# Four generator units per visit, lower products three tiles behind, and one adapter visit per block in a four-stage float32 kernel

## The chip, the cores and the metric

The kernel runs on one core of a Trainium2 chip. The metric is device time in microseconds (us) from launch to end: the median of several runs. One further run was taken under the hardware profiler; all durations below come from that one. The core has five engines that run side by side, each with its own queue worked through in order: PE (matrix products), DVE (vector), ACT (scalar functions), POOL (a second vector engine, which also issues stores here) and SP, which only issues DMA transfers.

## The reference

4096 tokens of width 256 (64 sequences of 64), a condition vector of 64 numbers per sequence, and four layers in a row. Cut to what matters:

```python
# layer 0: normed, gated up product, then quantized ternary down product
h = x * ((cond @ norm_w.T + 1)[:, None] * rsqrt(mean(x*x) + 1e-6))
val, gate = split(h @ up_w.T)                  # up_w: 2048 x 256
y = act_quant(val * gelu(gate)) @ weight_quant(down_w).T + x
# layer 1: attention and a gated MLP, both scaled by vectors made of the condition
x = x + (t @ attn_alpha_w.T)[:, None] * attention(ada_rmsnorm(x, t, attn_gamma_w, attn_beta_w))
x = x + (t @ ffn_alpha_w.T)[:, None] * swiglu(ada_rmsnorm(x, t, ffn_gamma_w, ffn_beta_w))
# layer 2: layer norm plus tanh(condInfo @ lin_w.T + lin_b)
# layer 3: an adapter whose two weights are generated for each sequence
Wd_b = Wd + ((h_lang @ Wdd.T + bdd) * 0.1).reshape(B, 128, 256)
Wu_b = Wu + ((h_lang @ Wdu.T + bdu) * 0.1).reshape(B, 256, 128)
out  = x + relu(x @ Wd_b.T + bd) @ Wu_b.T + bu
```

The generated weights are 64 times two matrices of 32,768 numbers: 16.8 MB of generator weights are read, and as much is written to device memory and read back.

## The kernel before

Precision is kept by splitting each float32 operand of a large product into a high and a low part; `mm3` (lines 81 to 85) makes three products of them. Apart from SP's, the order of each engine's work is the order in which the program is written out: whatever the Python loop emits first comes first in that engine's queue. SP's order is chosen by a scheduler. Tiles come from pools with a fixed number of buffers per tag; taking a buffer again waits for its last reader.

**Stage 0** (`l0`, lines 288 to 507) runs over 32 tiles of 128 tokens, eight blocks of four. For tile `n`, `upper(n, 0)` and `upper(n, 1)` each make 12 products of 128x512 into two of the eight PSUM banks (tag `mm`), then ACT's gelu (line 395) and a DVE product (396). `quant(n)` (399) is five DVE instructions and a DMA transpose issued by SP into `qt`. `lower(n)` (412) is eight bf16 products from `qt` and two DVE instructions. In the loop at line 473 `lower` is two tiles behind `upper`, with tiles 0 and 1 both at `n == 3`. `ternary` and `ternary_rest` (321, 326) quantize the down weights at `n` 1 and 2; a DVE sum of two ACT results is line 328, and PE's line 330 needs it.

Beside that the stage does the **generator**, 32 units: `gen_load` (257, SP loads 512 KB into one of four `gt` buffers), `gen_make` (266, four products of 64x64 weights by 512 columns into two banks) and `gen_store` (277, two ACT copies into one of two `stg` buffers, two stores issued by POOL). Two units are made before the loop, then two per even tile.

`cond_rest` (134, a hook of tile 4) makes seven condition vectors: 14 products of 64 rows (line 116) and two of 256 columns (151), all on partitions 0 to 63.

**Attention** follows and is not touched. **The last stage** (line 1066 on) runs over 64 visits, `n = 8*i + f` for block `i`: `f_inner(n)` is 24 products of 128x512, `f_outer(n - 2)` 12 of 128x256, each with ACT and DVE work between. For the next block, `f_load`, `f_begin` (ACT squares, line 210, and a POOL root) and `f_scale` (four ACT instructions, line 225) run at `f` 2, 3 and 4, and PE's transposes of the result (line 234) at 5 and 6. For the block before, the adapter's down product `f_down(i - 1)` (858, 64 records on PE) is at `f == 6` and its up product `f_up_products(i - 1)` (873) at `f == 7`. Both use the two `mm` banks of this stage. `f_weights` loads the generated weights at `f == 6`. The last block's adapter is in `f_last`.

The loop of stage 0 and its ends are what the change moves most:

```python
                if n % 2 == 0 and n > 0:
                    gen_make()
                    gen_make()
                    gen_load()
                    gen_load()
                    gen_store()
                    gen_store()
...
            if n == 3:
                lower(0)
            if n >= 3:
                lower(n - 2)
```

Of the kernel before, what the change touches and what calls it, by code (L numbers as in the profile page):

```python
# [28 lines left out]
X1 = 5  # L29
# [7 lines left out]
def tile_kernel(ctx: ExitStack, tc, xT, x, condT, cw, upT, downT, qkvT, woT, ghT, outT_w,  # L37
# [87 lines left out]
    def cond_load():  # L125
        nc.sync.dma_start(out=vc, in_=vecs)
        bo = crest["bo"] = main.tile([NB, D], F32, tag="xg", bufs=2, name="bo")
        nc.sync.dma_start(out=bo, in_=rows[0:1, :].broadcast_to([NB, D]))
        for v0 in (1, 5):
            n = min(4, 8 - v0)  # L130
            cwt = crest[v0] = main.tile([64, 4, D], F32, tag="x1", bufs=X1, name=f"cwt{v0}")
            nc.sync.dma_start(out=cwt[:, :n], in_=cw[:, v0:v0 + n, :])

    def cond_rest():
        part = const.tile([P, 1], mybir.dt.int32, name="part")
        nc.gpsimd.iota(part, pattern=[[0, 1]], base=0, channel_multiplier=1)
        pbit = const.tile([P, 1], mybir.dt.int32, name="pbit")
        nc.vector.tensor_scalar(pbit, part, 16, None, ALU.bitwise_and)
        pf = const.tile([P, 1], F32, name="pf")
        nc.vector.tensor_copy(pf, pbit)  # L140
        nc.vector.tensor_scalar(par[:, 1:2], pf, 1.0 / 16.0, None, ALU.mult)
        nc.vector.tensor_scalar(par[:, 0:1], pf, -1.0 / 16.0, 1.0, ALU.mult, ALU.add)
        nc.vector.tensor_tensor(w2, vc[:, 1, :], vc[:, 1, :], ALU.mult)
        bo = crest["bo"]
        al = main.tile([NB, 3, D], F32, tag="xn", bufs=1, name="al")
        pbs = [bank("mm") for _ in range(3)]
        for v0 in (1, 5):
            for v in range(v0, min(v0 + 4, 8)):
                cond_vector(crest[v0][:, v - v0], pbs[v0 // 5], 2 * NB * (v - v0))
        for i, v in enumerate((V_AA, V_FA)):  # L150
            nc.tensor.matmul(pbs[2][:NB, i * D:(i + 1) * D], lhsT=ct[0:64], rhs=crest[1 + 4 * i][:, v - 1 - 4 * i],
                             start=True, stop=True)
        src = [pb.rearrange("p (v c b) -> p v c b", c=2, b=NB) for pb in pbs]
        nc.vector.tensor_copy(cv[:, 1:5], src[0])
        nc.vector.tensor_copy(cv[:, 5:7], src[1][:, 0:2])
        nc.vector.tensor_copy(al[:, 0:2], pbs[2][:NB].rearrange("b (i d) -> b i d", i=2))

        th = main.tile([P, 2, NB], F32, tag="st", bufs=2, name="th")
        for c in range(2):
            nc.scalar.activation(th[:, c], src[1][:, 2, c], AF.Tanh, bias=vc[:, 3, c:c + 1])  # L160
        nc.vector.tensor_tensor(al[:, 2], al[:, 1], bo, ALU.mult)
        nc.gpsimd.dma_start(out=alphad.rearrange("v b d -> b v d"), in_=al)
        for c in range(2):
            nc.vector.tensor_scalar(th[:, c], th[:, c], vc[:, 2, c:c + 1], vc[:, 1, c:c + 1], ALU.add, ALU.mult)
            nc.vector.tensor_scalar(cv[:, V_LIN, c], th[:, c], vc[:, 2, c:c + 1], None, ALU.add)
# [88 lines left out]
    gen_left = [(g, sd, k) for g, sd in ((g1, s1d), (g2, s2d)) for k in range(16384 // (2 * GC))]  # L254
    gen_loaded, gen_made = [], []

# [19 lines left out]

    def gen_store():
        if gen_made:
            pb, dst = gen_made.pop(0)
            uid[0] += 1  # L280
            stg = pools["a"].tile([P, 2, GC], F32, tag="stg", bufs=2, name=f"stg{uid[0]}")
            for s in range(2):
                nc.scalar.copy(stg[:, s], pb[s])
            for c in range(2):
                nc.gpsimd.dma_start(out=dst[:, :, c * GC:(c + 1) * GC], in_=stg[c * 64:(c + 1) * 64])


    def l0(hooks):
# [32 lines left out]
        def ternary():  # L321
            for j in range(2):
                wj = main.tile([P, 4, D], F32, tag="xn", bufs=1, name=f"wj{j}")
                nc.scalar.activation(wj, til["wd"][j], AF.Abs, accum_out=sa[:, j:j + 1])

        def ternary_rest():
            wd, ones = til.pop("wd"), til.pop("ones")
            nc.vector.tensor_tensor(sb[:, 0:1], sa[:, 0:1], sa[:, 1:2], ALU.add)
            pb = bank("mm")
# [69 lines left out]
        def quant(n):  # L399
            h = til[n]  # L400
            am = pool.tile([P, 4], F32, tag="am", bufs=4, name=f"am{n}")
            nc.vector.tensor_reduce(am[:, 0:1], h, AX.X, ALU.max, apply_absolute_value=True)
# [4 lines left out]
            nc.vector.tensor_scalar(q, h, -MAGIC, 127.0, ALU.add, ALU.min)  # L407
            qt = pool.tile([P, 8, P], BF16, tag="qt", bufs=3, name=f"qt{n}")
            nc.sync.dma_start_transpose(out=qt, in_=q)
# [26 lines left out]
        load_up(3, nc.sync)  # L436
        gen_load()
        load_up(1, nc.sync)
        gen_load()
        til["ones"] = pool.tile([P, P], F32, name="ones")  # L440
# [18 lines left out]
        nc.vector.tensor_scalar(gl, ct, 0.1, None, ALU.mult)  # L459
        gen_make()  # L460
        gen_make()
        for j in (3, 1):
# [4 lines left out]
        upper(1, 0, "rest")  # L467
        gen_store()
        gen_store()
        gen_load()  # L470
        gen_load()
        N = NBLK * TT
        for n in range(N + 2):
            if n < N:
                if n > 1:
                    upper(n, 0)
                if n % 2 == 0 and n > 0:
                    gen_make()
                    gen_make()
                    gen_load()  # L480
                    gen_load()
                    gen_store()
                    gen_store()
# [18 lines left out]
            if n < N - 1:  # L502
                quant(n)
            if n == 3:
                lower(0)
            if n >= 3:
                lower(n - 2)

# [286 lines left out]

    def f_weights(i):

        pool = pools["c"]
        B = fblk[i]
        B["wd"], B["wu"] = [], []  # L800
        for k in range(2):
            bs = slice(i * BB + 4 * k, i * BB + 4 * k + 4)
            wd = pool.tile([P, 4, 2, BN], F32, tag="wd", bufs=4, name=f"wd{i}_{k}")
            for c in range(2):
                nc.sync.dma_start(out=wd[:, :, c, :], in_=s1d[c, bs].rearrange("b d n -> d b n"))
            wu = pool.tile([P, 4, D], F32, tag="wu", bufs=4, name=f"wu{i}_{k}")
            for s in range(2):
                nc.sync.dma_start(out=wu[s * 64:(s + 1) * 64], in_=s2d[s, bs].rearrange("b n d -> n b d"))
            B["wd"].append(wd)
            B["wu"].append(wu)  # L810

# [51 lines left out]

    def f_up_products(i, half=None):
        B = fblk[i]
        b0, b1 = (0, BB) if half is None else (half * BB // 2, (half + 1) * BB // 2)
        pus = []
        for c in range(2):
            pu = bank("mm" if half is None else "gh")
            for b in range(b0, b1):  # L870
                for s in range(2):
# [4 lines left out]
                                     tile_position=(0, 64 * s))  # L876
            pus.append(pu)
        return pus

    def f_up_store(i, pus, half=None):  # L880
        B = fblk[i]
        if half in (None, 0):
            B["yo"] = pools["c"].tile([P, 2, T], F32, tag="yo", bufs=1, name=f"yo{i}") if i + 1 < NBLK else \
                main.tile([P, 2, T], F32, tag="xn", bufs=1, name=f"yo{i}")
        yo, n = B["yo"], T if half is None else T // 2
        o = 0 if half is None else half * n
        for c in range(2):
            nc.vector.scalar_tensor_tensor(yo[:, c, o:o + n], pus[c][:, :n], vc[:, 4, c:c + 1], B["x4"][:, c, o:o + n],
# [177 lines left out]
    for n in range(5, N):  # L1066
        i, f = divmod(n, 8)
        ahead = 0 < i < NBLK - 1

# [8 lines left out]
        if i > 0 and f in (4, 5):  # L1078
            f_adapt(i - 1, f - 4)
        if i + 1 < NBLK and f in (5, 6):  # L1080
            late = [norm_turn(*fblk[i + 1]["n"], i + 1, f - 5, V_FG, V_FB)]
        if ahead and f == 6:
            f_down(i - 1)
        if ahead and f == 7:
            pus = f_up_products(i - 1)
        f_parts(n, sg)
        f_outer(n - 2) if n > 5 else None
        if ahead and f == 7:
            f_up_store(i - 1, pus)
        if n == 6:  # L1090
            for k in range(2):
                nc.vector.scalar_tensor_tensor(bias[:, k], gbt[:, 2 * k + 1], 0.1, gbt[:, 2 * k], ALU.mult, ALU.add)
        if i > 0:
# [5 lines left out]
            if f == 2:  # L1099
                f_center(i - 1, range(TT), rln)  # L1100
        if f == 2 and i > 0:
            f_rows(i)
            if i + 1 < NBLK:
                f_load(i + 1)
        if i > 0 and i + 1 < NBLK:
            if f == 3:
                f_begin(i + 1)
            if f == 4:
                f_scale(i + 1)

        if f == (6 if i + 1 < NBLK else 2):
            f_weights(i)
        if i + 1 < NBLK and f == 7:
            f_common(i, "wd", 0)
# [3 lines left out]
        if i > 0 and f in (3, 4):  # L1118
            f_common(i - 1, "wu", f - 3)
        if i + 1 == NBLK:  # L1120
            if f == 4:
# [61 lines left out]
```

## Time and profile before

| | us |
|---|---|
| three runs | 772.38, 776.98, 777.23 (median 776.98) |
| the profiled run | 779.7 |
| its span, from first to last instruction | 777.9 |
| stage 0, to the first attention products | about 282 |
| DVE busy, whole span | 545.4 (70%) |
| ACT busy | 398.8 (51%) |
| POOL busy | 336.8 (43%) |

The profile has a page of sums, and the trace behind it answers questions: busy time of each engine by stretch, with the clock that PE was granted; the list of who waited for whom; and each engine's instructions in order of time. In a row of such a list, the first number is the start in us, the second how long it took (several equal instructions in a row are merged, `x16` being their number), and the bracket at the end is the idle time before it and what ended it. A PE record's duration contains its way through the array; the pace of PE is the distance between the starts of neighbouring records. One float32 product of 64-row or 64-column tiles is two records.

### The profile page before, as it was taken

To read this page: it belongs to the slowest core of one execution; us is meant where nothing else is said; L and a number is where in the kernel's file an instruction comes from. 1 tells how busy PE (TensorE), PEld (TensorE's weight loads), DVE (VectorE), ACT (ScalarE), POOL (GpSimd) and SP (SyncE) were. 2 spreads that over 40 slices of the span, in tenths; PEclk is the share of its full clock that TensorE was granted. 3 is DMA by queue.
4 is the path that set the end of the run, shared out by engine and by line. 5 is a ranking of instruction groups with operands and counts; after the bars stand their busy time and mean duration, and the time that the engine had idled before them with its cause. 6 is when DMAs were issued, how large, how long until landed. Compare 5 with 4: busy or idle time off the path is not lost. (4 is left out here: it accounts for less than half of the span.)

```text
span 777.9 us, 17431 instructions
## 1 busy us (share of the span) xinstructions
PE 757.5 (97%) x7034; PEld 618.7 (80%) x7034; DVE 545.4 (70%) x863; ACT 398.8 (51%) x818; POOL 336.8 (43%) x348
## 2 busy tenths in 40 slices
PE   8989999999999999999999999999999999999997
PEld 5667767776776878888888888888888888888886
DVE  4868687786778689898889886555555555564665
ACT  6624355344354478888887674534444352526232
POOL 2312122221324336566655417381818272636491
PEclk9989999999999999999999999999999999999999
DMA  8966888987974774455654127726161617171601
GB/s 309 322 173 201 235 244 220 299 193 223 289 187 114 194 173 103 128 142 136 151 150 110 46 93 176 163 77 142 56 163 56 163 55 163 55 163 32 160 1 56
DMA packets 117184, 118.87 MB, mean 153 GB/s; under 512 B 39616, under 2 KB 100672, under 8 KB 117104
## 3 DMA queue, kind: packets, MB, share of 16 engines
q1 hardware_dynamic: 109104, 91.55, 48.1%
q0 software_dynamic: 7488, 25.37, 9.1%
q8 instruction: 55, 0.90, 0.5%
q10 hardware_dynamic: 512, 0.85, 0.4%
q14 instruction: 25, 0.20, 0.1%
HBM read 71.41 MB, written 29.56 MB: 130 GB/s over the span
## 5 line engine op out<-in xcount | busy, mean ns | idle before, releaser
L83 PE MATMUL mm<-up,xhl 128*128 128x512 f32 x256 | 107.2, 419 | 1.4 <-ACT xhl L217 1.4
L730 DVE TENSOR_TENSOR sg<-gh,sg 128x512 f32<-128x512 f32 x61 | 42.0, 689 | 93.5 <-ACT sg L729 47.4
L84 PE MATMUL mm<-up,xhl 128*128 128x512 f32 x256 | 102.5, 400 | 0.4 <-DVE up L313 0.4
L85 PE MATMUL mm<-up,xll 128*128 128x512 f32 x256 | 102.4, 400 | 0.0
L83 PE MATMUL gh<-xhf,gh 128*128 128x512 f32 x244 | 97.2, 399 | 0.0
L84 PE MATMUL gh<-xlf,gh 128*128 128x512 f32 x244 | 96.9, 397 | 0.0
L85 PE MATMUL gh<-xhf,gh 128*128 128x512 f32 x244 | 96.9, 397 | 0.0
L395 ACT ACTIVATE g<-mm,rs_l 128x512 f32<-128x512 f32 x64 | 43.9, 689 | 89.0 <-PE mm L85 65.3
L752 DVE TENSOR_TENSOR hlo<-sg,hhi 128x512 fp32r<-128x512 f32 x61 | 63.1, 1034 | 37.0 <-ACT hhi L751 36.6
L751 ACT CAST hhi<-sg 128x512 fp32r<-128x512 f32 x61 | 37.8, 620 | 84.7 <-DVE sg L730 83.8
L396 DVE SCALAR_TENSOR_TENSOR h<-mm,rs_l,g 128x512 f32<-128x512 f32 x64 | 47.5, 747 | 44.2 <-PE mm L85 43.1
L83 PE MATMUL acc<-wout,hhi 128*128 128x256 f32 x256 | 74.9, 293 | 0.0
L85 PE MATMUL acc<-wout,hlo 128*128 128x256 f32 x256 | 72.4, 283 | 0.3 <-DVE hlo L752 0.2
L84 PE MATMUL acc<-wout,hhi 128*128 128x256 f32 x256 | 72.3, 282 | 0.0
L83 PEld LDWEIGHTS mm<-up,xhl 128*128 128x128 f32 x256 | 49.2, 192 | 25.0 <-DVE am L404 4.9
L729 ACT ACTIVATE sg<-gh 128x512 f32<-128x512 f32 x61 | 36.0, 590 | 53.1 <-PE gh L85 53.1
L85 PEld LDWEIGHTS mm<-up,xll 128*128 128x128 f32 x256 | 48.8, 191 | 12.2 <-DVE xll L218 0.3
L84 PEld LDWEIGHTS mm<-up,xhl 128*128 128x128 f32 x256 | 49.2, 192 | 10.7 <-DVE up L313 0.9
L85 PEld LDWEIGHTS gh<-xhf,gh 128*128 128x128 f32 x244 | 46.1, 189 | 10.8
L238 POOL TENSOR_TENSOR xg<-xg,cv 128x512 f32<-128x512 f32 x32 | 35.8, 1128 | 42.9 <-DVE xg L237 42.9
L84 PEld LDWEIGHTS gh<-xlf,gh 128*128 128x128 f32 x244 | 46.3, 190 | 8.1
L83 PEld LDWEIGHTS gh<-xhf,gh 128*128 128x128 f32 x244 | 46.3, 190 | 8.1
(189 smaller groups left out, 1882.4 us busy)
## 6 DMA issues: line engine op xcount, KB each, us to landing
gt<-in_g SPq DMA_DIRECT2D x32, 512.0 KB, 5.8
rows<-alphad SPq DMA_DIRECT2D x48, 256.0 KB, 4.3
s1d<-stg POOLq DMA_DIRECT2D x32, 256.0 KB, 6.9
s2d<-stg POOLq DMA_DIRECT2D x32, 256.0 KB, 6.6
vb<-vx SPq DMA_DIRECT2D x32, 256.0 KB, 4.7
wd<-s1d SPq DMA_DIRECT2D x32, 256.0 KB, 4.5
wu<-s2d SPq DMA_DIRECT2D x32, 256.0 KB, 6.2
xt<-in_x SPq DMA_DIRECT2D x8, 512.0 KB, 5.3
```

Source lines behind the costliest of these rows:

```text
L83: nc.tensor.matmul(out, lhsT=l[0], rhs=r[0], start=first, stop=False)
L84: nc.tensor.matmul(out, lhsT=l[0], rhs=r[1], start=False, stop=False)
L85: nc.tensor.matmul(out, lhsT=l[1], rhs=r[0], start=False, stop=last)
L238: nc.gpsimd.tensor_tensor(b3(xg), b3(xg), bc(vb, c, i), ALU.add)
L395: nc.scalar.activation(g, pg, AF.Gelu, scale=rs[:, t:t + 1])
L396: nc.vector.scalar_tensor_tensor(h[:, ch * 512:(ch + 1) * 512], pv, rs[:, t:t + 1], g, ALU.mult, ALU.mult)
L729: nc.scalar.activation(sg, pg, AF.Silu)
L730: nc.vector.tensor_tensor(sg, pv, sg, ALU.mult)
L751: nc.scalar.copy(h_hi, sg)
L752: nc.vector.tensor_tensor(h_lo, sg, h_hi.bitcast(F32), ALU.subtract)
```

## The change

Generator: none is made before the loop; eight visits, at tiles 5, 8, 11, 15, 18, 22, 25 and 29, make four units each, with their ACT copies right behind (`gen_stage`, four staging buffers from two pools instead of two). Loads and stores are called once per tile (twice at some visits). `lower` runs three tiles behind instead of two. The condition weights lie on both halves of the partitions, and the products alternate between the halves. The sum of line 328 moves from tile 2 to tile 1. In the last stage the up product of block `i - 2` and the down product of block `i - 1` are one visit at `f == 7`, the down product between the two halves of the up product; preparation of the next block moves to `f` 0, 1 and 3, and weights are loaded at `f` 6 (down) and 7 (up).

```diff
+        cwt = crest["w"] = main.tile([P, 4, D], F32, tag="x1", bufs=X1, name="cwt")
+        nc.sync.dma_start(out=cwt[0:64], in_=cw[:, 1:5, :])
+        nc.sync.dma_start(out=cwt[64:128, 0:3], in_=cw[:, 5:8, :])
...
-        for v0 in (1, 5):
-            for v in range(v0, min(v0 + 4, 8)):
-                cond_vector(crest[v0][:, v - v0], pbs[v0 // 5], 2 * NB * (v - v0))
+        pbs = [bank("mm") for _ in range(4)]
+        for k in range(4):
+            for c in range(2):
+                for h in range(2 if k < 3 else 1):
+                    hs = slice(64 * h, 64 * h + 64)
+                    nc.tensor.matmul(pbs[h][:, (2 * k + c) * NB:(2 * k + c + 1) * NB],
+                                     lhsT=cwt[hs, k, c * P:(c + 1) * P], rhs=ct[hs], start=True, stop=True)
+        for h, k in ((0, V_AA - 1), (1, V_FA - 5)):
+            hs = slice(64 * h, 64 * h + 64)
+            nc.tensor.matmul(pbs[2 + h][:NB, :D], lhsT=ct[hs], rhs=cwt[hs, k], start=True, stop=True)
...
+    def gen_stage():
+            gen_turn.append(pools["kv"] if len(gen_turn) % 2 else pools["a"])
+            stg = gen_turn[-1].tile([P, 2, GC], F32, tag="stg" if len(gen_turn) % 2 else "qf", bufs=2,
                                    name=f"stg{uid[0]}")
             for s in range(2):
                 nc.scalar.copy(stg[:, s], pb[s])
+            gen_staged.append((stg, dst))
...
+            nc.vector.tensor_tensor(sb[:, 0:1], sa[:, 0:1], sa[:, 1:2], ALU.add)
...
         def ternary_rest():
-            nc.vector.tensor_tensor(sb[:, 0:1], sa[:, 0:1], sa[:, 1:2], ALU.add)
...
+        visits = (5, 8, 11, 15, 18, 22, 25, 29)
-                if n % 2 == 0 and n > 0:
-                    gen_make()
-                    gen_make()
+                if n in visits:
+                    for _ in range(4):
+                        gen_make()
+                        gen_stage()
+                for _ in range(0 if n == 0 else 2 if n in visits and (n + 3 in visits or n == visits[-1]) else 1):
                     gen_load()
-                    gen_load()
-                    gen_store()
                     gen_store()
...
-            if n == 3:
-                lower(0)
-            if n >= 3:
-                lower(n - 2)
+            if n > 3:
+                for k in range({4: 0, N + 1: N - 1}.get(n, n - 3), {N: N - 1, N + 1: N}.get(n, n - 2)):
+                    lower(k)
...
-        ahead = 0 < i < NBLK - 1
+        more = i + 1 < NBLK
...
-        if ahead and f == 6:
-            f_down(i - 1)
-        if ahead and f == 7:
-            pus = f_up_products(i - 1)
+        up = i - 2 if more and f == 7 else i - 2 if not more and f == 0 else -1
+        if up >= 0:
+            def between(pus):
+                f_up_store(up, pus, chunks=range(1))
+                if more:
+                    f_down(i - 1)
+            pus = f_up_products(up, between=between)
+            f_up_store(up, pus, chunks=range(1, 2))
+        elif more and i > 0 and f == 7:
+            f_down(i - 1)
...
+            if f == 0:
+                f_load(i + 1)
+            if f == 1:
+                f_begin(i + 1)
+            if f == 3:
+                f_scale(i + 1)
...
-        if f == (6 if i + 1 < NBLK else 2):
-            f_weights(i)
+        if f == (6 if more else 1):
+            f_weights(i, "wd")
+        if f == (7 if more else 1):
+            f_weights(i, "wu")
```

The two buffer counts that go with it: `am` 5 instead of 4, `qt` 4 instead of 3. The two `gen_load` calls between the first weight loads are gone.

## The prediction

> **What bounds the kernel.** First the table of busy time by stretch. Its columns are the stretch, then time on PE (records), PE's weight loads, DVE, ACT and POOL, the clock granted to PE, DMA share and GB/s.
>
> ```profile
> 40.00:60.00 20.00, 17.63 (x95) 12.47 (x93) 12.63 (x31) 3.96 (x8) 3.23 (x6) 0.84 0.68 172
> ...
> 120.00:160.00 40.00, 40.00 (x212) 28.83 (x213) 31.88 (x59) 16.78 (x34) 6.88 (x11) 1.00 0.87 242
> ...
> 560.00:600.00 40.00, 39.86 (x320) 34.52 (x320) 21.37 (x35) 16.61 (x35) 20.21 (x18) 1.00 0.42 106
> ```
>
> PE is full almost everywhere, so only two things can be won: PE's few waits, and PE time that does no work. From 40 to 60 us PE waits 2.4 us and its clock averages 0.84. Cut into single microseconds, the clock is at 0.50 or falling to it from 43.5 to 46.9 and from 57.1 to 60.5: twice 3.4 us at half pace, 1.7 us lost each time.
>
> Next, who PE and its weight loads waited for (total, times, longest):
>
> ```profile
> PE mm L421 <- DMA qt<-q: 2.4, 1, 2.4
> ...
> PE mm L330 <- DVE sb L328: 1.4, 1, 1.4
> ...
> PEld mm L234 <- ACT xnf L225: 3.1, 12, 0.3
> ```
>
> Then PE in order of time, at those waits and at the two kinds of narrow products:
>
> ```profile
> 42.85 1.33 PE L421 MATMUL mm<-wq,qt 128*128 128x256 bf16 x8 [2.37 <-DMA qt<-q]
> ...
> 53.06 3.34 PE L116 MATMUL mm<-ct,cwt 64*128 64x64 f32 x28
> 56.32 1.22 PE L151 MATMUL mm<-cwt,ct 64*64 64x256 f32 x4
> 57.48 1.89 PE L421 MATMUL mm<-wq,qt 128*128 128x256 bf16 x8
> ...
> 68.85 0.40 PE L85 MATMUL mm<-up,xll 128*128 128x512 f32 x1
> 69.17 1.95 PE L273 MATMUL mm<-gt,gl 64*64 64x512 f32 x16
> 71.05 0.50 PE L83 MATMUL mm<-up,xhl 128*128 128x512 f32 x1
> 71.39 0.39 PE L84 MATMUL mm<-up,xhl 128*128 128x512 f32 x1
> ```
>
> ```profile
> 591.67 0.60 PE L234 MATMUL mm<-ident,xnf 128*128 128x128 f32 x4
> 592.20 2.08 PE L858 MATMUL mm<-x,wd 128*64 128x64 f32 x64
> 594.21 0.38 PE L83 MATMUL acc<-wout,hhi 128*128 128x256 f32 x1
> 594.43 0.28 PE L84 MATMUL acc<-wout,hhi 128*128 128x256 f32 x1
> ```
>
> Going into narrow products and out again costs time beside the work. Wide 128x512 products start 0.233 us apart; from 68.85 to 71.39 is 2.54, less two wide steps 2.07. The sixteen records in it start in four groups, 0.43 apart, so the work is 1.72 and the switching **0.36**. From 591.67 to 594.43 is 2.76; four transposes at 0.108, 32 pairs of records at 0.058 and one product at 0.117 make 2.41, the rest is **0.35**.
>
> **The change, part by part.**
>
> *Generator visits.* Sixteen become eight; products, copies, loads and stores stay the same in number. 8 x 0.36 = **2.9** won. A visit of four takes 4 x 0.86 + 0.36 = 3.8 on PE, and its eight copies on ACT 8 x 0.515 = 4.1 (four merged are 2.06). A visit fills all eight banks. In the program, the last two units and the products after them wait for copies of the first three, one copy or so behind, and for DVE's reads of the tile. DVE, at 80% here, is at most one `quant` (3.1) behind while PE has two units (1.7) and the tile's own second half (2.8) to do. I take no wait; if PE had to stand until every copy is out, it would be 1.0 (first unit) + 4.1 - 3.8 = 1.3 a visit, 10.4 in all.
>
> The Trainium skill speaks against this part (TensorEngine Tiling (Array Packing), PSUM Bottleneck): tiling speeds TensorE but not the emptying of PSUM, whose copies can become the bound. By it the visits would run at the pace of the copies, 0.33 longer each, and the change would win 2.6 less.
>
> *Loads and stores.* In SP's order in the changed program the four loads of a visit stand almost together, behind the visit whose buffers they take; transposes queue behind them, but the next `lower` is then still two tiles (over 12 us) away, against 5.8 to land a load and 3.7 a transpose. The stores have two more staging buffers. At the start, two loads fewer stand ahead of the last up weights and four ahead of the down weights, so these only come earlier. 0.
>
> *Line 328 a tile earlier.* At tile 2 it stood behind `quant(1)` and two products on DVE. Now it waits there for ACT's two sums, which end near 24; PE asks near 28. The gap from 31.77 to 33.52 less one step: **1.5**.
>
> *`lower` three behind.* Tile 1's transpose gets one more tile, and the 2.37 wait goes: **2.4**. The half clock right behind it goes too: **1.7**.
>
> *Condition vectors.* From the last wide step (52.97) to 57.48 is 4.5. Single records start 0.112 apart, the four 256-column ones about 0.22. That quarters of the array run at once is shown by the generator's groups of four, which start within 0.02. Two halves at once: 14 x 0.112 + 2 x 0.22 + 0.5 for switching = 2.6, so **1.9** won (0 to 2.0).
>
> *A new wait, tiles 4 and 5.* Without the early generator work PE runs ahead of DVE. PE from 16.7: eight half tiles at 2.8, the `ones` product 0.2, condition 2.6, two `lower` 1.7: at 43.5 it wants a bank of `upper(4, 0)`. DVE from 20.3 without a pause: `quant(0)` 3.1, a product 0.7, the next block's split 2.8, `quant(1)` 3.1, two products 1.4, ternary 4.7, `quant(2)` 3.1, two products 1.4, `quant(3)` 3.1, one product 0.7: 44.4. **-0.9**. If the pairing saves nothing, PE comes 1.9 later and this wait is gone, so the two terms together are 0 to 2 and I take 1.0. Behind the wait stand the first generator visit and all of PE; from tile 8 on DVE has caught up.
>
> *The second half clock.* It came after some 4 us in which PE was never idle, but at most half of the array had work. Only 2.6 such us are left: **1.7**, or 0.
>
> The skill (TensorE: Matmul & The Clock Gate, Part 1) gives half rate as the state after an idle window of about 3.4 us. This trace differs: one drop came after 2.4 us of waiting, one after none. By the page, long visits could never cost clock.
>
> *Last stage.* Twelve adapter visits become seven: 5 x 0.35 = **1.8**. The up product's second half needs the bank of its first back: DVE finishes the inner product (0.7) and reads the bank (0.7) while PE spends 1.9 on the down product. The relu on ACT now waits for the up product's end, since `dn` has one buffer, and `hhi` stands behind it, 4 us late; `f_outer` reads that two visits (8 us) later. The normed rows (line 225) move to `f == 3`, a visit of 4.2 before PE's transposes instead of right ahead of them; ACT is 42% busy there and the POOL root is one visit earlier as well. The 3.1 of waits go: **3.1**. What is then latest is PE itself.
>
> Sum: 2.9 + 1.5 + 2.4 + 1.7 + 1.0 + 1.7 + 1.8 + 3.1 = **16.1**. From the profiled run's 779.7 (span 777.9) that makes 763.6 (761.8). The profiled run is 2.7 above the median of the plain runs, 776.98, so for those: **761**.
>
> **Rivals.**
>
> *Half of it* (0.14). The second drop stays (1.7), pairing brings nothing (1.0), and the normed rows' wait is replaced by another of its size in the last stage (3.1): 10.3 won, 767. For it: a block there has three DVE chains close to PE. Against: those rows alone are listed for PE's loads.
>
> *Banks bind* (0.08). PE stands until copies are out: 16.1 - 10.4 = 5.7 won, 771. For it: eight copies need 4.1 against PE's 3.8. Against: copies free banks one by one, and 15 waits of ACT for generator products (21.8 us) stand against two of PE for copies (1.6, weight loads only).
>
> *Long visits cost clock* (0.06), the slower case. A visit of 3.8 us and an adapter visit of 1.9 + 1.9 = 3.8 are both longer than the 3.4 us of a drop. If narrow tiles count as little work, each of the 8 + 7 is followed by half clock: 15 x 1.7 = 25.5, net 9.4 lost, 786. It decides from the tenth drop on (16.1 / 1.7). For it: the drop at 57.1 followed narrow products. Against: those used one half and were spaced by weight loads; generator records fill four quarters back to back, and no drop follows any of sixteen visits.
>
> *It does not do what it says*: the four loads are not spread over the tiles, as SP's order shows; that costs nothing by the sum above.
>
> **How the numbers follow.** The forecast has 0.72. The range reaches from 756 (no new wait, and a run like the 772.38 one) to 769 (half of it, and a little more): both first cases, about eight in ten. Runs before lie 4.9 apart, so 1% (7.8 us) is about what can be told from no change. Faster by more: 0.72 + 0.14 less 0.02 for drift = 0.84. Within 1%: the bank case and the drift, 0.10. Slower: 0.06.
>
> **What would show it.** Right: no PE wait for `qt` or `sb` and none of `xnf`; no 0.50 clock between 40 and 65; eight generator visits of 3.8; condition records starting in pairs; seven adapter visits; one PE wait near 1 us for DVE's `h` at tile 5; the first attention products some 10 us sooner. Wrong: PE waiting for `stg` at the visits, half clock behind them, or idle DVE while PE waits for `qt`.

## The result and the profile after

The changed kernel takes **768.89 us** (median of seven runs, 766.15 to 770.52). The kernel before, run beside it on the same chip, takes 773.41 (seven runs, 772.38 to 777.23). The ratio on record is 0.992, with a 95% interval of 0.9891 to 0.9949 (the quotient of the two medians is 0.994). The forecast was 761, with 769 as its upper end: the sign was right, but 0.8% was won where 2.1% was forecast. The profiled run of after took 768.89, its span 767.1.

The table of busy time by stretch, for the changed kernel, with the columns of the first table above:

```profile
40.00:60.00 20.00, 19.50 (x132) 13.40 (x131) 18.73 (x41) 8.94 (x17) 4.62 (x7) 1.00 0.62 171
120.00:160.00 40.00, 40.00 (x225) 27.87 (x224) 30.27 (x58) 20.49 (x46) 9.79 (x15) 1.00 0.95 244
200.00:240.00 40.00, 37.09 (x198) 25.20 (x200) 28.32 (x53) 18.63 (x47) 12.26 (x17) 0.96 0.90 206
560.00:600.00 40.00, 40.00 (x340) 35.21 (x339) 22.36 (x36) 16.83 (x36) 21.11 (x18) 1.00 0.48 114
```

The early stretch is mended: PE is busy for 19.50 of 20 us where it was 17.63, at a clock of 1.00 where it was 0.84. But a new hole stands at 200 to 240, where PE is short by 2.9 us and the clock is at 0.96. The list of waits names it:

```profile
PE mm L278 <- DVE x L435: 2.9, 2, 2.0
```

Line 278 is the generator's product, line 435 the last instruction of `lower` on DVE, which frees the bank that the generator wants. PE in order of time, first at the condition vectors, then at the visit of tile 25:

```profile
41.06 2.00 PE L152 MATMUL mm<-ct,cwt 64*128 64x64 f32 x28
42.98 0.65 PE L156 MATMUL mm<-cwt,ct 64*64 64x256 f32 x4
43.56 1.92 PE L434 MATMUL mm<-wq,qt 128*128 128x256 bf16 x16
45.99 0.50 PE L83 MATMUL mm<-up,xhl 128*128 128x512 f32 x1 [0.51 <-DVE h L409]
...
48.98 3.84 PE L278 MATMUL mm<-gt,gl 64*64 64x512 f32 x32
...
198.02 1.05 PE L434 MATMUL mm<-wq,qt 128*128 128x256 bf16 x8
201.80 2.81 PE L278 MATMUL mm<-gt,gl 64*64 64x512 f32 x24
206.58 1.47 PE L278 MATMUL mm<-gt,gl 64*64 64x512 f32 x8 [1.97 <-DVE x L435]
```

A visit of four takes 3.84 here, where nothing holds it, and 3.66 at the five visits that follow. At tile 25 three units take 2.81, then PE waits 1.97 for the bank of the `lower` at 198.02, and its clock is at 0.50 from 207.2 to 210.6. What kept DVE from reading that bank is in DVE's own order:

```profile
200.72 0.75 DVE L418 TENSOR_SCALAR h<-h,am 128x1024 f32<-128x1024 f32 x1
205.12 0.69 DVE L420 TENSOR_SCALAR q<-h 128x1024 bf16<-128x1024 f32 x1 [3.65 <-DMA qt<-q]
205.73 0.21 DVE L431 TENSOR_SCALAR am<-am,sb 128x1 f32<-128x1 f32 x1
206.04 0.48 DVE L435 SCALAR_TENSOR_TENSOR x<-mm,am,xt 128x256 f32<-128x256 f32 x1
```

Line 420 writes `q` of tile 24. There are two `q` buffers, so it waits until the transpose of tile 22 has read its own. That transpose by itself, issued by SP at 189.2, with who waited for it and the time from issue to landing:

```profile
L422 SPq DMA_TRANSPOSE qt<-q x1: 4775/4775/4775, 189.2 to 189.2; - x1
...
  DVE q L420: 3.7, 1
...
DMA to landing us min/median/max: 15.8/15.8/15.8
```

A tile takes 6.5 us on PE, so `q` comes round after 13.0: a transpose that lands within some 12 us costs nothing, one of 15.8 stops DVE.

The other of the two waits, at tile 29, is not the work of a transpose. These are rows of PE, DVE and POOL:

```profile
239.46 1.94 PE L278 MATMUL mm<-gt,gl 64*64 64x512 f32 x14 [0.94 <-DVE x L435]
```

```profile
237.05 1.64 DVE L420 TENSOR_SCALAR q<-h 128x1024 bf16<-128x1024 f32 x1
```

```profile
236.57 1.58 POOL L223 TENSOR_TENSOR xla<-xg,xha 128x512 fp32r<-128x512 f32 x1 [0.73 <-ACT xha L222]
```

Line 420 waits for nothing there, but takes 1.64 instead of 0.69 while POOL works on line 223. Of the 32 writes of `q` in this profile, the two slow ones (1.64 and 1.67) are the two that stand beside that line; whether the one causes the other was not tried. PE's wait at tile 29 is 0.94 or 0.95 in all five profiled runs with that visit and two `q` buffers, and 0.60 with three.

The stages, cut in the trace at the first transposes of `ex` (line 625 before, 632 after; a few attention products lie ahead of them) and at the first product of the last stage: stage 0 ends at 281.8 before and 279.1 after, the attention stage lasts 171.1 and 168.0, and the rest 325.0 and 320.1. The attention stage is the same code in both kernels; it lasts 168.0 to 171.1 in the sixteen profiles of this document, so its 3.1 are no gain of the change.

### The profile page after: what moved, and what is told of

Same layout as the page of the kernel before. It is cut to its first block, busy times and chain, and to the rows that moved or that the text cites. A ratio compares the mean times of both kernels' runs of the same rounds, so it can differ in the third digit from the quotient of the medians.

```text
span 767.1 us, 17409 instructions
## 1 busy us (share of the span) xinstructions
PE 750.2 (98%) x7034; PEld 618.9 (81%) x7034; DVE 546.7 (71%) x864; ACT 396.3 (52%) x818; POOL 339.4 (44%) x348
## 4 chain that ended last, share of the span: by engine, by line
PE 84%; DVE 7%; DMA 4%; issue 3%; ACT 1%; POOL 0%; SPq 0%; DVEq 0%; POOLq 0%; ACTq 0%
PE mm L83 10%; PE mm L84 10%; PE mm L85 10%; PE gh L83 7%; PE gh L84 7%; PE gh L85 7%; PE acc L83 4%; PE acc L85 4%; PE acc L84 4%; PE mm L278 3%; PE mm L434 3%; PE mm L632 2%; PE S L591 2%; PE mm L239 2%; DMA qt<-q 2%
## 5 line engine op out<-in xcount | busy, mean ns | idle before, releaser
L759 DVE TENSOR_TENSOR hlo<-sg,hhi 128x512 fp32r<-128x512 f32 x61 | 58.5, 959 | 31.2 <-ACT hhi L758 30.2
## 6 DMA issues: line engine op xcount, KB each, us to landing
rows<-alphad SPq DMA_DIRECT2D x48, 256.0 KB, 4.3
s1d<-stg POOLq DMA_DIRECT2D x32, 256.0 KB, 9.6
s2d<-stg POOLq DMA_DIRECT2D x32, 256.0 KB, 6.6
vb<-vx SPq DMA_DIRECT2D x32, 256.0 KB, 4.6
wd<-s1d SPq DMA_DIRECT2D x32, 256.0 KB, 6.4
wu<-s2d SPq DMA_DIRECT2D x32, 256.0 KB, 6.4
```

Source lines behind the costliest of these rows:

```text
L759: nc.vector.tensor_tensor(h_lo, sg, h_hi.bitcast(F32), ALU.subtract)
```

## The experiments

Each run lists its own median beside runs of the kernel before on the same chip: "ratio" is to those, as on record, and up to 0.2% from the quotient of the two medians. Spans and stages are from each run's one profile. The first DVE product of tile 0 comes at 16.1 to 18.2 us in these profiles, so up to 2 us of a difference in "stage 0 ends" lie in the start.

| run | median us (runs) | before there | ratio, 95% | stage 0 ends | rest |
|---|---|---|---|---|---|
| before again | 776.69 (8) | 774.47 | 1.001, 0.999 to 1.0031 | 279.0 | 324.9 |
| last stage alone | 771.06 (10) | 774.47 | 0.9941, 0.9921 to 0.9961 | 277.8 | 320.0 |
| all but last stage | 772.38 (10) | 774.47 | 0.998, 0.9954 to 1.0005 | 276.1 | 325.0 |
| third `q` buffer | 765.76 (4) | 774.47 | 0.9881, 0.9849 to 0.9912 | 273.1 | 320.0 |
| after again | 771.16 (5) | 776.22 | 0.9932, 0.9903 to 0.996 | 278.3 | 320.0 |
| generator as before | 764.78 (4) | 776.22 | 0.986, 0.9832 to 0.9888 | 273.0 | 320.0 |
| visits four tiles apart | 762.62 (4) | 776.22 | 0.9828, 0.9801 to 0.9855 | 270.3 | 321.0 |
| both edits | 762.64 (4) | 776.22 | 0.9829, 0.9797 to 0.9862 | 272.0 | 320.1 |
| sixteen visits of two | 766.66 (4) | 776.76 | 0.9881, 0.9859 to 0.9904 | 275.1 | 320.1 |
| visits three tiles apart | 764.24 (4) | 776.76 | 0.9853, 0.983 to 0.9876 | 272.6 | 320.7 |
| `lower` and line 328 alone | 773.39 (12) | 776.76 | 0.9967, 0.9947 to 0.9988 | 280.5 | 325.0 |
| condition vectors alone | 772.3 (12) | 776.76 | 0.9949, 0.9933 to 0.9965 | 275.8 | 325.0 |
| fewer stores at tile 22 | 766.26 (2) | 777.43 | 0.9858, 0.9815 to 0.9901 | 275.5 | 320.0 |
| more stores at tile 18 | 766.91 (2) | 777.43 | 0.9866, 0.9803 to 0.993 | 276.2 | 320.4 |

### The kernel before, profiled again

> The kernel before, unchanged, profiled once more. Theory 'rare events in the one profile': the 2.4 us wait of PE for qt, the two half clocks between 40 and 65 us, and the four waits of 4.2 us in the attention stage belong to the run of 779.7 and not to the kernel; then some of them are missing here and the span is some 4 to 6 us shorter (772 to 774). Rival 'they belong to the kernel': all of them recur, the time is 776 to 780, and the whole shortfall of the change lies in the kernel after.

Two of PE's waits in its first 100 us, and then the table by stretch where the clock fell (the clock is the third number from the right):

```profile
PE mm L330 <- ACT junkl L210: 1.3, 1, 1.3
PE mm L421 <- DMA qt<-q: 0.6, 1, 0.6
```

```profile
54.00:56.00 2.00, 2.00 (x12) 1.31 (x11) 1.37 (x4) 0.52 (x2) 0.01 (x1) 0.69 0.81 221
56.00:58.00 2.00, 2.00 (x6) 1.52 (x5) 1.93 (x5) 0.00 (x0) 0.63 (x1) 0.50 0.75 252
```

The wait for `qt` is 0.6, not 2.4, and no half clock follows it; the half clock behind the narrow products recurs (54.8 to 58.2); the attention stage's four waits of 4.2 are three of 1.7. Span 772.8, against 777.9. So the first theory holds for most of it. Aligning the DVE product of each tile shows how sharp the division is: from tile 8 to 28, this run, the run of the prediction and the run with the last stage alone keep their distances to each other within 0.03 us. All that differed in stage 0 of this code lies before tile 6.

### Halves of the change

The first kernel is the one before with the diff's hunks from `f_weights` on, the second the one after without them. The core of these hunks:

```diff
-        if ahead and f == 6:
-            f_down(i - 1)
-        if ahead and f == 7:
-            pus = f_up_products(i - 1)
+        if up >= 0:
+            def between(pus):
+                f_up_store(up, pus, chunks=range(1))
+                if more:
+                    f_down(i - 1)
+            pus = f_up_products(up, between=between)
...
+            if f == 0:
+                f_load(i + 1)
```

> The kernel before with the edits of the last stage alone. If the last stage's terms are right (five visits fewer 1.8, no wait for the normed rows 3.1), it is 4.9 us faster than before, about 768.5 beside 773.4, and the time between the first attention products and the end is all that changes. Rival: the waits for the normed rows come back elsewhere, and it wins 1.8 only (771.6).

Measured: 0.9941, that is 4.6 us, and in the trace the time from the start of the last stage to the end is 320.0 against 324.9: **4.9**, the two terms to a tenth. The trace of after shows the new visit, up product, down product, up product, with nothing idle between:

```profile
586.36 1.15 PE L882 MATMUL mm<-dn,wu 128*64 128x64 f32 x32
587.34 2.04 PE L866 MATMUL mm<-x,wd 128*64 128x64 f32 x64
589.21 1.11 PE L882 MATMUL mm<-dn,wu 128*64 128x64 f32 x32
```

> The kernel after with the last stage of before. By the terms on record stage 0 should win 11.2; by the two traces it wins 2.7 (282.1 to 279.4). Theory 'held transposes': the gain by tile 24 is there and is lost at the visits of tiles 25 and 29, so this run wins 2 to 4 us (769 to 771) and its trace shows DVE waiting for the transpose at a late visit. If stage 0 wins 8 or more here, the two traces misled.

Measured: 772.38, ratio 0.998: about 1.5 us won, at the low end and hardly told from nothing. At tile 25 PE waited 0.81 here, without a half clock. So all that misses the forecast is in stage 0.

### A third buffer for `q`

```diff
...
-            stg = gen_turn[-1].tile([P, 2, GC], F32, tag="stg" if len(gen_turn) % 2 else "qf", bufs=2,
...
+            if gen_turn[-1]:
+                stg = pools["kv"].tile([P, 2, GC], F32, tag="qf", bufs=2, name=f"stg{uid[0]}")
+            else:
+                stg = pools["kv"].tile([P, 4, GC], F32, tag="vb", bufs=2, name=f"stg{uid[0]}")[:, :2]
...
-            q = pool.tile([P, FF], BF16, tag="q", bufs=2, name=f"q{n}")
+            q = pool.tile([P, FF], BF16, tag="q", bufs=3, name=f"q{n}")
```

> The kernel after with three q buffers in place of two (the staging buffers move to memory that is free in this stage); visits, loads, stores and copies are unchanged. Theory 'held transposes': line 420 stood 3.65 us at tile 24 for the transpose of tile 22, which took 15.8 us to land among the loads and stores of a visit, and so line 435 was late for PE. With a third buffer line 420 does not wait, PE's waits at line 278 (2.9 us) and the half clock behind the first (1.7) go, and the time is 4 to 5 us less than after: 764 to 765. Rival 'copies bind': PE's waits at the visits are due to eight copies on ACT against PE's 3.8 us; then nothing changes (768 to 769).

The transpose of tile 22 (line 424 in this kernel), and then DVE at tile 24 (line 422 writes `q`):

```profile
L424 SPq DMA_TRANSPOSE qt<-q x1: 2956/2956/2956, 187.3 to 187.3; - x1
...
DMA to landing us min/median/max: 14.1/14.1/14.1
```

```profile
198.83 0.75 DVE L420 TENSOR_SCALAR h<-h,am 128x1024 f32<-128x1024 f32 x1
199.61 0.69 DVE L422 TENSOR_SCALAR q<-h 128x1024 bf16<-128x1024 f32 x1
```

The transpose is as late as ever (14.1), and DVE does not notice. PE's waits at the visits fall from 2.9 to 0.6, all of it at tile 29, the clock stays at 1.00, and the time is 765.76: by the two ratios some 3 us less than the kernel after, where 4 to 5 were expected. The chain transpose, `q`, line 435, bank, PE is shown for tile 25. ACT still makes eight copies a visit, so they are not what bound.

### The generator as before, and the kernel after once more

```diff
+        gen_make()
+        gen_make()
...
-                if n in visits:
-                    for _ in range(4):
-                        gen_make()
-                        gen_stage()
+                if n % 2 == 0 and n > 0:
+                    gen_make()
+                    gen_make()
```

> The kernel after with the generator as before: two units ahead of the loop, two in every even tile, two staging buffers. Lower three behind, line 328, paired condition vectors and the last stage stay as in the kernel after. Theory 'held transposes': bunched visits win 2.9 by fewer switches and lose 3.9 at tile 25 and 0.8 at tile 29 plus 0.5 at tile 5, so this run is 0 to 3 us faster than the kernel after (766 to 769 beside 769). Rival 'the visits pay, the rest does not': then this run is 2.9 slower than the kernel after, about 772.

> The kernel after, unchanged. From tile 8 on the three runs of before's stage 0 kept the same distances to 0.01 us, so what differs between runs is the start and the narrow products of the first 60 us. Theory: the waits at the visits of tiles 25 and 29 recur (2.9 and 1.7 us in the two runs seen), the half clock behind tile 25 only where its wait was 2.0; time 767 to 770, 0.8% under before.

On the same chip 764.78 and 771.16: **taking the generator edit out of the change makes it 6.4 us faster**, more than was expected. Without it the change wins 1.4%. The kernel after, run again, repeats its waits (4.0 in all, 3.10 of them at tile 25). The transpose of tile 22 took 16.9 there, and 14.1 to 16.9 in the four profiled runs with these visits and this order of stores. One part of the expectation fell: no half clock came behind the 3.10; this profile has it at 8 to 15 us and at 315 to 319 instead.

### Visits spaced otherwise

```diff
-        visits = (5, 8, 11, 15, 18, 22, 25, 29)
+        visits = (3, 7, 11, 15, 19, 23, 27, 30)
...
-                for _ in range(0 if n == 0 else 2 if n in visits and (n + 3 in visits or n == visits[-1]) else 1):
+                for _ in range(2 if n in (2, 27, 30, 31) else 1):
```

```diff
-        visits = (5, 8, 11, 15, 18, 22, 25, 29)
+        visits = (5, 8, 11, 14, 17, 20, 23, 26)
```

The first puts visits four tiles apart but for the last, the second three. The calls of `gen_load` and `gen_store` follow the visits, so that four units are loaded and stored between two of them; the stores are thereby called in another order too, and these runs do not try spacing by itself. A third kernel makes sixteen visits of two units (tiles 4, 5, 7, 9, 10, 12 and so on to 29), with loads held back while four units wait. "Both edits" joins the visits four tiles apart with the third `q` buffer.

> The kernel after with its eight visits at tiles 3, 7, 11, 15, 19, 23, 27, 30, four tiles apart but for the last, in place of 5, 8, 11, 15, 18, 22, 25, 29; nothing else is changed. Theory 'held transposes', as a matter of spacing: four loads and eight stores then have 26 us and not 23, no transpose is held long enough, and the 2.0 wait with its half clock (3.9 in all) at the visit of tile 25 is gone without a new buffer: 764 to 766. Rival, phase: what holds the transposes is the visit's meeting with the block's own transfers (store of x1, load of xt and of ax), and visits at every fourth tile meet them each time or never; then the waits are in several visits (770 or more).

> Both edits, three q buffers and visits four tiles apart. If each removes the same wait, the two together win no more than one alone, 764 to 766; if late visits still lose 0.8 with three q buffers because DVE is behind there, spacing removes that too, 763 to 765. It should be the fastest of all.

Measured: 762.62 and 762.64. PE's waits in stage 0 of the first, complete down to 0.3:

```profile
PE mm L444 <- POOL nhalf L98: 1.4, 1, 1.4
PE mm L84 <- DVE up L326: 1.2, 1, 1.2
PE mm L239 <- DVE xna L232: 0.8, 1, 0.8
PE mm L632 <- DVE xg L242: 0.5, 1, 0.5
PE mm L83 <- DVE x L435: 0.3, 1, 0.3
```

No generator product waits. Transposes still take up to 11.7 at these visits, inside the 12 or so that are free. The third buffer adds nothing to that. This version beats both kernels: 1.7% under before, and 8.5 us under the kernel after on the same chip.

> The kernel after with all eight visits three tiles apart (5, 8, 11, 14, 17, 20, 23, 26): the suspected cost is doubled. Theory 'held transposes, spacing': the transfers of a visit need more than the 23 us of three tiles, the backlog is not worked off in between, and from the third gap on most visits find a late transpose: three to five waits of 1 to 3 us, 3 to 10 us slower than the kernel after (772 to 780). Rival 'phase': only a visit in the tile where the block's own transfers start holds the next one; then one or two waits as now, 767 to 771.

> The kernel after with sixteen visits of two units (tiles 4, 5, 7, 9, 10, 12 and so on to 29) in place of eight of four; all else is as in the kernel after. By the sum on record eight more switches cost 2.9, and by the theory of held transposes the 3 to 4 us lost at tile 25 and 0.8 at tile 29 go: 1 to 2 us faster than the kernel after, and 2.9 slower than the run with eight visits four tiles apart. In its trace no PE wait for line 435. Rival 'long visits': if visits of four units are what fills the banks, this run equals the run four tiles apart.

Three tiles apart is **not** worse than the kernel after: 764.24, no PE wait for line 435, and no transpose seen over 12.9. That brought down the explanation by spacing. Sixteen visits of two took 766.66; their stage 0 ends 4.9 later than with the visits four apart: eight more switches at 0.36 are 2.9 of it, the first tile came 1.1 later, and the rest lies within the 1.3 that PE is listed as waiting for DVE's `h` in the early tiles.

### What held the transpose: the stores in POOL's queue

```diff
+                k = 0 if n == 0 else 2 if n in visits and (n + 3 in visits or n == visits[-1]) else 1
+                late = {22: 1, 23: 1, 24: 2}.get(n, k)
+                for m in range(2):
+                    if m < k:
+                        gen_load()
+                    if m < late:
+                        gen_store()
```

```diff
-        visits = (5, 8, 11, 15, 18, 22, 25, 29)
+        visits = (5, 8, 11, 15, 18, 21, 25, 29)
```

> The kernel after with one change in the order of POOL's queue: at tile 22 the stores of one unit instead of two, at tile 24 those of two instead of one. Theory 'burst of stores': the transpose of tile 22 lands in under 12 us (at tile 18, with this order, it took 5.2 and that of tile 19 took 7.3), no DVE wait at line 420, no PE wait for line 435 at tile 25 but for a few tenths: 3 to 4 us faster than the kernel after. Rival 'whatever the order of stores': the transpose takes 14 to 17 us again and PE waits 1 to 3 us.

> The kernel after with the visit of tile 22 moved to 21, so that tile 18 is the visit followed by one three tiles later, with the stores of two units in its own tile, as tile 22 had. Theory 'burst of stores': the transpose of tile 18 takes 14 to 17 us, DVE waits at line 420 of tile 20, and PE waits 1 to 3 us at the visit of tile 21. Rival: no transpose over 13 us and no such wait, and the time is 764 to 766, as in the run with all visits three tiles apart.

First POOL's order at tile 22 in the kernel after, then in the run with fewer stores there:

```profile
181.02 2.39 POOL L298 DMA_DIRECT2D s2d<-stg  x4 [15.71 <-ACT stg L291]
...
190.22 0.81 POOL L437 DMA_DIRECT2D x1d<-x  x1 [1.70 <-DVE x L435]
191.04 2.42 POOL L298 DMA_DIRECT2D s2d<-stg  x4
```

```profile
181.12 1.20 POOL L298 DMA_DIRECT2D s2d<-stg  x2 [15.71 <-ACT stg L291]
...
190.32 0.81 POOL L437 DMA_DIRECT2D x1d<-x  x1 [1.70 <-DVE x L435]
191.14 4.06 POOL L298 DMA_DIRECT2D s2d<-stg  x6
```

In POOL's order two stores of 256 KB have moved behind the store of `x1`, nothing else. The transpose of tile 22 in that run, and DVE at tile 24:

```profile
DMA to landing us min/median/max: 10.1/10.1/10.1
```

```profile
201.60 0.69 DVE L420 TENSOR_SCALAR q<-h 128x1024 bf16<-128x1024 f32 x1
```

10.1 instead of 15.8, and no wait. In the other kernel the burst was moved to tile 18, whose transpose took 5.2 in the kernel after, with SP's loads in the same order around it; the two rows are its transpose and DVE at tile 20:

```profile
DMA to landing us min/median/max: 15.2/15.2/15.2
```

```profile
173.97 0.69 DVE L420 TENSOR_SCALAR q<-h 128x1024 bf16<-128x1024 f32 x1 [3.06 <-DMA qt<-q]
```

So the burst of four stores at a visit, followed by the block's own store of `x1`, is what held the transpose of tile 22, and it holds that of tile 18 when it is put there: shown from both sides for these two tiles. The times follow only in part (766.26 and 766.91): the moved burst cost PE 1.4 at tile 21 and no half clock.

The Trainium skill says (DMA: Bandwidth & Descriptors, Issuing engines are not separate DMA queues) that transfers end up on the same 16 DMA engines and interleave, whichever engine started them. That agrees: with two stores fewer ahead of it on POOL's queue, a transpose on SP's queue landed 5.7 us sooner.

Left open: the burst does not hold every transpose. In the run with visits three tiles apart, tile 14 has the same four stores, `x1`, four stores on POOL, and the transposes of tiles 14 and 15 took 5.4 and 8.0. Its stores go to `s1d`, those at 18 and 22 to `s2d`; whether that matters was not tried.

### The early parts alone

Both are the kernel before, the first with these lines, the second with the diff's hunks of `cwt` and `cond_rest` and nothing else:

```diff
+            nc.vector.tensor_tensor(sb[:, 0:1], sa[:, 0:1], sa[:, 1:2], ALU.add)
...
-            am = pool.tile([P, 4], F32, tag="am", bufs=4, name=f"am{n}")
+            am = pool.tile([P, 4], F32, tag="am", bufs=5, name=f"am{n}")
...
-            qt = pool.tile([P, 8, P], BF16, tag="qt", bufs=3, name=f"qt{n}")
+            qt = pool.tile([P, 8, P], BF16, tag="qt", bufs=4, name=f"qt{n}")
...
-            if n >= 3:
-                lower(n - 2)
+            if n > 3:
+                for k in range({4: 0, N + 1: N - 1}.get(n, n - 3), {N: N - 1, N + 1: N}.get(n, n - 2)):
+                    lower(k)
```

> The kernel before with lower three tiles behind and line 328 a tile earlier, nothing else. On record these terms are 1.5 + 2.4 + 1.7 = 5.6. In three runs of before's stage 0 the wait for qt was 2.4, 0.6 and under 0.2 us, and only the first had a half clock behind it. Theory 'rare events in the one profile': it wins 1.5 to 2.5 (0.2 to 0.3%). If it wins 4 or more, the terms were right.

> The kernel before with the paired condition vectors alone. The term on record is 1.9 without the new wait, as the generator's early units are still there, and 1.7 more where the half clock behind the narrow products goes (it came in two of three runs of before's stage 0): 2 to 3.5 faster (0.25 to 0.45%). Rival: DVE is so close behind in tiles 4 and 5 that PE waits there for what it won: 0 to 0.5.

Measured: 2.6 us (0.9967) and 4.0 us (0.9949). The first is just above what the rare-events theory gives (1.5 to 2.5) and well under the 5.6 on record. The second is above its range (2 to 3.5): 2.0 are the pairs, and the half clock that is gone would be 1.7 more. Between 50 and 61 us that half clock came in three of four profiled runs with unpaired vectors (in the alone run of `lower` it lasted 6.8 us), and in none of twelve with paired ones.

## Why the prediction fell short

The parts, measured alone, are 2.6 + 4.0 + 4.6 = 11.2 us; the change without the generator edit won 10.9 (776.22 at 0.986). They add up. The generator edit was forecast to win 2.9, and lost 4.7 to 6.4.

Where that went can be read from the profiles, counted from the first DVE product of tile 0 to the end of stage 0, so that the start does not enter. The kernel after takes 261.2 (again: 260.8), the generator as before 256.0. Two runs with the visits of the kernel after, in which no transpose holds PE at tile 25, take 257.0 (third `q` buffer) and 257.4 (fewer stores): the held transpose is 3.3 to 4.1. Even so these two take 1.0 to 1.4 more than the generator as before, with waits of 0.6 to 0.9 at tile 29 and 0.5 at tile 5 in their lists. Visits three tiles apart take 255.4, visits four tiles apart 254.2.

- **Loads and stores, "0": the step that failed.** It said that transposes queue behind the loads, but the next `lower` is over 12 us away. It guarded the wrong reader. The first to need the transpose is not `lower`, with four `qt` buffers, but `quant` two tiles on, with two `q` buffers; and the price of a transpose was taken as 3.7, its usual one, where it took 15.8 under the burst. In place of 0 the term is a loss of 3.3 to 4.1. The stores were passed in one sentence on staging buffers, without POOL's order, in which the block's `x1` store stands between two bursts. SP's order was looked at; the same look at POOL's order would have shown the burst.
- **Generator visits, 2.9 and "no wait": half right.** The switches are worth somewhat less than was said: 2.2 by the medians of the generator as before and of visits four tiles apart. The copies never bound, and a free visit took 3.66 to 3.84 against 3.8. By the Trainium skill (TensorEngine Tiling (Array Packing), PSUM Bottleneck) each visit would have been 0.33 longer; in the row at 48.98 it is not, and the measurement decides. But banks did make PE wait, through DVE, whose lag was bounded at one `quant` (3.1) without a wait of DVE's own: 1.97 at tile 25, and 0.94 at tile 29 without any late transpose. The rival "banks bind" had the place and not the cause.
- **`lower` three behind, 2.4 + 1.7: mis-sized, counted from one run.** Three profiles of that code waited 2.4, 0.6 and under 0.2, and one had the half clock. With line 328 these terms were 5.6 and measured 2.6. The prediction knew that its profiled run was 2.7 above the median and subtracted that from the total, but left the rare events in the sum.
- **Line 328, 1.5:** the wait of 1.3 to 1.4 is gone from every run with the edit.
- **Condition vectors, 1.9, new wait -0.9, second half clock 1.7:** 43.56 - 41.06 = 2.5 against 2.6; the wait is there, at the product named, 0.51; the half clock is gone.
- **Last stage, 1.8 + 3.1:** 4.9 by the traces.
- **Long visits cost clock:** fell. Six of the eight visits ran unbroken, and no half clock follows them, nor the one at tile 29, which waited 0.94; the one at tile 25 followed a wait of 1.97.

Of the signs of being wrong, the half clock came behind a visit, once, and PE did wait at two visits, though for line 435 and not for `stg`. Of the signs of being right, the first attention products came 2.7 sooner and not some 10. With the visits four tiles apart the same plan wins 13.4 of the 16.1 forecast (762.6 against 776.2): the sum is nearly right where no transpose is held. In part that is luck, as errors in it cancel: the terms of `lower` and line 328 fall 3.0 short, while the condition vectors, measured alone, win 4.0, where 2.7 were taken for them together with a new wait that these visits do not have.

## What to carry to other kernels

When transfers are bunched, look for the buffer with the fewest copies that a transfer reads or writes, and compare its round (here two tiles, 13 us) with the longest landing time under the bunch (here 16.9), not the median (3.7 before); follow every queue, the one that issues stores too. Before summing terms from one profile, ask of each wait whether it recurs: work that is placed the same in three runs to 0.03 us can be trusted, a wait on a transfer in the first tiles cannot. A change of several parts can win overall while one part loses: take each part out once.

## What the runs showed of the hardware

The half clock does not follow the length of one wait: it came after 2.0 (tile 25) and 2.4 us (before), and not after 3.1 (after again, tile 25). Its length was 3.4 us or twice that, and in three profiled runs with narrow products in half of the array it came without PE being idle at all. The Trainium skill (TensorE: Matmul & The Clock Gate, Part 1) describes a free-running window of 3413 ns, and half rate after an idle one; the lengths agree, the drop without an idle PE does not follow from it, nor do those after waits shorter than the window.

In the first 15 us, where PE waits up to twice for the operands of its first up products, the sixteen profiles part cleanly: where the waits add up to 2.93 us or more (five profiles), 6.8 us of half clock stand there; where they add up to 2.67 or less (eleven), none.

Transposes of 256 KB took 2.7 us (before) to 16.9 us (after again) from issue to landing. The transpose of tile 22 alone took 14.1 to 16.9 with the burst of stores ahead of it and 10.1 with two stores fewer.
